# Keys spread by transfers, one bank of scores shared with POOL, and transposes moved in the queue

## The chip, the core and the metric

The kernel runs on one core of a Trainium2 chip. The metric is the device time of one execution in microseconds (us), lower is better. Three executions of the kernel before took 1627.0, 1628.25 and 1634.33 us, so the median is 1628.25 us. A fourth execution was profiled: it took 1626.31 us, of which 1624.5 us lie between its first and its last instruction (the span of the profile).

The five engines are named as the profile names them: PE (matrix products and transposes), DVE, ACT and POOL (elementwise work; POOL can't read the accumulators, DVE and ACT can), and SP, which here issues nearly all transfers. Each engine works through its own queue in order. All numbers are float32.

## The reference

Four layers follow each other on `x` of 128 batches by 64 tokens by 128 channels, with a second input of the same shape as context. The first three hold five attentions between them, all of the same form, with 16 heads of 8 channels (`HD`):

```python
def attend(q, k, v):                    # (batch, head, token, 8)
    a = softmax(einsum('bhnd,bhsd->bhns', q, k) * 8 ** -0.5, axis=-1)
    return einsum('bhns,bhsd->bhnd', a, v)
x = x + gate * (attend(q(xn), k(xn), v(xn)) @ proj + bias)   # "self", gated
x = x + attend(q(xn), k(c), v(c)) @ proj + bias              # "cross"
```

Layer 0 has a self attention (called L0s in the code), a cross attention (L0c) and an MLP; layer 1 is a cross attention with both sides modulated (L1c); layer 2 is self attention, cross attention (L2s, L2c) and MLP; layer 3 has attention with a single head and routed experts, and is not touched by the change.

## The kernel before

**Tiling.** The 8192 tokens are 16 groups of 512 (8 batches). `x` stays in SBUF (`xs`). Each attention runs over the 16 groups; L0s and L0c are one list of 32 groups, and L1c, L2s and L2c one list of 48, so that one attention runs into the next. A group is worked in two halves of four batches, `u = 0` and `u = 1`. Each half is one step of `attend` (line 571), so there are 160 halves.

**One half.** `scores` (468) makes the scores of 4 batches and 16 heads on PE: `sc`, 128 partitions by 2048, which fills four banks of PSUM. It has one buffer, so the next half's scores wait until this half's have been read. DVE takes the maximum over each row of 64 keys (`mx`, 485) and subtracts it (`e`, 487). `turned` (493) transposes half of `e` in 16 PE instructions into `pp`, two banks with one buffer, and ACT takes the exponential into `eT` (507). It is called twice in a half. `weighted` (509) multiplies by the values (`po`, 520), and ACT copies the product to `o` (528). A half passes through a pipeline: at each step the scores are of this half, the transposes of the last, the weighted sum of the one before.

**Preparation of a group** (`prepare`, 386) is a generator, cut into eight pieces by its `yield`s: load of context, statistics, normalization on POOL (372), transposes of the key input (`psT`, 342) with their evacuation by ACT (eight pieces of 128x64 where the layer modulates by batch, 359; otherwise one copy, 379), the same for the query input of a cross attention, keys, queries (`pq`, 449, to `qT`, 451), values (`pvv`, 459, to `vbd`, 464 and 465). The keys are `pk` (436), which ACT writes to `kT` (438); POOL then multiplies them by four masks (444) into `kbd`: of each block of 32 channels, that is 4 heads, `kbd[:, j]` holds the 8 channels of head `j` and zeros elsewhere. That lets one product per block of 32 rows give the scores of four heads.

**Finish of a group** (`finish`, 530) sends the denominators (which came out of `weighted` as additional columns of ones in `vbd`) through DRAM (`sums`, 538; `rc`, 542), moves the odd heads' rows of `o` beside the even ones by four transfers (545), takes reciprocals (547), sends them through DRAM (`recs`, 549) and back as one row per channel (`rb`, 554), multiplies on POOL (`oT`, 557), projects (`py`, 563) and adds to `x` (565, or 568 and 569 with a gate from the table `gt`, 278).

**What sets the order.** The order is written out by hand in `step` (588): after the first transposes and the weighted sum, an even step (`u = 0`) runs one piece of the finish of group i-2, of the preparation of i+4 and i+1 (keys), of the finish of i-3 (projection), then the second transposes, then a piece of the preparation of i+2 (`psT`) and i+3. On PE this gives for an even step: `sc`, `pp`, `po`, `pk`, `py`, `pp`, `psT`; for an odd one: `sc`, `pp`, `po`, `pq`, `pp`, `pvv`, and `psT` of the query input in a cross attention. Two PSUM buffers (pool `mm`, line 139) serve `po`, `pk`, `py`, `psT`, `pq` and `pvv` in turn. The first and last steps of a list are interleaved with the MLPs (`into_mlp`).

Of the kernel before, what the change touches and what calls it, by code (L numbers as in the profile page):

```python
# [15 lines left out]
P = 128  # L16
NST = 16
TT = 4
# [17 lines left out]
for _name, _n in _VECS:  # L36
# [13 lines left out]
    "L3_xcond_router_W": (3, 3), "L3_xcond_e_w1": (9, 256), "L3_xcond_e_w2": (6, 128),  # L50
    "L3_xcond_gate_w1": (3, 128), "L3_xcond_gate_w2": (1, 128), "L3_xcond_out_w": (1, 128),
}
_RAW = [
    "x", "cond_1024", "ctx_1024", *_WTS,
    "L0_xcond_ca_proj_b", "L1_xcond_bp", "L2_xcond_b_cproj", "L3_xcond_router_b", "L3_xcond_e_b2",
# [4 lines left out]
def tile_kernel(ctx: ExitStack, tc: tile.TileContext, a: dict, out: bass.AP):  # L60
# [15 lines left out]
    nc.sync.dma_start(cond, a["cond_1024"])  # L76
    vec_rows = const([_NVEC, P], "vec_rows")
    nc.scalar.dma_start(vec_rows, a["vecs"])
    mask = const([P, 4], "mask")
    nc.scalar.dma_start(mask, a["mask"])  # L80

    w = {}

    def load_weights(prefix, pool=cp):
        for name, (k, n) in _WTS.items():
            if name.startswith(prefix):
                t = pool.tile([P, k, n], F32, tag=name, name=name)
                src = a[name]
                if len(src.shape) == 3:
                    src = src.rearrange("e c n -> (e c) n")  # L90
                nc.sync.dma_start(t, src.rearrange("(k p) n -> p k n", p=P))
                w[name] = t

    xs = [const([P, TT, P], f"x{s}") for s in range(NST)]
# [23 lines left out]

    ident = const([P, P], "ident")
    make_identity(nc, ident)  # L120
    nhalf = const([P, TT], "nhalf")
    G.memset(nhalf, -0.5)

# [43 lines left out]
        Places.ak.tile([P, NB, 8, 32], F32, tag=f"vbd{i}", name=f"vbd{i}", bufs=1) for i in range(2)  # L167
    ]

    def clear(t):  # L170
        G.memset(t, 0.0)
        G.memset(t[0:L, :, :, 16:17], 1.0)
        G.memset(t[L:P, :, :, 17:18], 1.0)


# [2 lines left out]
    condT = const([P, P], "condT")  # L178
    scT = const([P, P], "scT")
    mods = {}  # L180

    def col(name, i=0):
        r = _ROW[name] + i
# [20 lines left out]

    def folded_column(wp, bp, bv, i):
        pb = mm("pb")
        T.matmul(pb[:, 0:1], w[wp][:, 0], col(bv, i), start=True, stop=True)
        t = const([P, 1], "pb_" + wp)
        V.tensor_add(t, pb[:, 0:1], col(bp))
        proj_bias[wp] = t  # L210
# [3 lines left out]
    def gate_table(wmod, wp, i=2, bias=None):  # L214

        table = dp.tile([P, 2, P], F32, tag="gate_" + wp, name="gate_" + wp)
        rows = const([P, 2, P], "gate_rows")
        gb = const([P, P], "gate_bias")
        V.tensor_scalar_mul(gb, mods[wmod][:, i, :], proj_bias[wp] if bias is None else bias)

        def second():
            pg = mm("pg")
            for q, src in enumerate((mods[wmod][:, i, :], gb)):
                T.transpose(pg[:, ts(q, P)], src, ident)
            V.tensor_copy(rows, pg[:, 0 : 2 * P].rearrange("p (i c) -> p i c", i=2))
            nc.sync.dma_start(table, rows)
            gates[wp] = table

        return second

    def folded_row(wp, bp, bv):
        bvs = const([P, P], "bvs")
        V.tensor_copy(bvs, col(bv, 1).broadcast_to([P, P]))

        def second():
            pb = mm("pb")
            T.matmul(pb[:, :P], bvs, w[wp][:, 0], start=True, stop=True)
            V.tensor_add(row_bias[bp], row_bias[bp], pb[:, :P])
            proj_bias[wp] = row_bias[bp]

        return second

    def condition():
        pc = mm("pc")
        T.transpose(pc[:, :P], cond, ident)
        V.tensor_copy(condT, pc[:, :P])
        S.activation(scT, pc[:, :P], AF.Silu)
        pv = mm("pv")
        T.transpose(pv[:, :_NVEC], vec_rows, ident[:_NVEC, :_NVEC])
        V.tensor_copy(vec, pv[:, :_NVEC])  # L250
        V.tensor_scalar_add(vec1, vec, 1.0)

    first_mods = modulations("L0_xcond_adaln_w", "L0_xcond_adaln_b", 6, (1, 4))
# [19 lines left out]
    def gate_tile(pool, s, wp):  # L273

        gt = pool.tile([P, TT, 2, P], F32, tag="gt", name="gt")
        for h in range(2):
            r = gates[wp].rearrange("(s t h) i c -> s h t (i c)", t=TT, h=2)[s, h]
            nc.sync.dma_start(
                gt[ts(h, L)].rearrange("p t i c -> p t (i c)"),
                r.unsqueeze(0).broadcast_to([L, TT, 2 * P]),  # L280
            )
        return gt

    later_tables = [
# [96 lines left out]

    turn = [0]

    ctxT = dp.tile([NST, P, NT], F32, tag="ctxT", name="ctxT")

    def prepare(pools, at):
# [16 lines left out]
        if cross:  # L403
            cn = c
            if layer != "L0c":
                cn = pool.tile([P, TT, P], F32, tag="cn", name="cn", bufs=1)
                for t in range(TT):
# [4 lines left out]
                    else:  # L412
                        S.activation(cn[:, t, :], c[:, t, :], AF.Identity, bias=nb, scale=rs)
        yield
        if layer == "L1c":
            kv_in = modulated_by_batch(pool, transposed(psum, cn), "L1_xcond_Wss_kv", 0, 1, s, "cm")
        elif cross:
            kv_in = copied(pool, transposed(psum, cn), "cm")
            if layer == "L0c":
                nc.sync.dma_start(ctxT[s], kv_in)  # L420
        else:
            q_in = kv_in = modulated_by_batch(
                pool, transposed(psum, xn), at["wmod"], 1, 0, s, by_dve=at.get("first", False)
            )
        yield
        if not cross:
# [12 lines left out]
        i = turn[0] % 2  # L439
        turn[0] += 1  # L440
        vbd = vbds[i]
        kbd = pool.tile([P, 4, NB, L], F32, tag="kbd", name="kbd")
        for j in range(4):
            (V if at.get("first") else G).tensor_scalar(  # L444
                kbd[:, j], by_batch(kT), mask[:, j : j + 1], 1.0, ALU.mult, ALU.mult
            )
        yield
        pq = psum.tile([P, 512], F32, tag="mm", name="pq")
        T.matmul(pq, at["wq"], q_in, start=True, stop=True)  # L449
# [11 lines left out]
                    start=True, stop=True,  # L461
                )
        pv4 = pvv.rearrange("p b (i d) -> p b i d", d=HD)
        S.copy(vbd[0:L, :, :, 0:HD], pv4[0:L])
        S.copy(vbd[L:P, :, :, HD : 2 * HD], pv4[L:P])
        at["vbd"] = vbd

    def scores(pools, at, u):
# [5 lines left out]
        for t2 in range(2):  # L474
# [9 lines left out]
        mx = pool.tile([P, 32], F32, tag="mx", name="mx")  # L484
        V.tensor_reduce(mx, sc.rearrange("p g (m k) -> p (g m) k", k=L), AX.X, ALU.max)  # L485
        e = pool.tile([P, 32, L], F32, tag="e", name="e")
        V.tensor_tensor(  # L487
            e, sc.rearrange("p g (m k) -> p (g m) k", k=L),
            mx.unsqueeze(2).broadcast_to([P, 32, L]), ALU.subtract,
        )  # L490
        return e

    def turned(pools, e, eT, gg):

# [35 lines left out]
    def finish(pools, at):  # L530
# [3 lines left out]
        cross = at["layer"][2] == "c"  # L534

        sums = dp.tile([16, NT], F32, tag="sums", name="sums", bufs=2)
        for j in range(2):
            nc.sync.dma_start(
                sums.rearrange("(g i j) t -> j g i t", i=2, j=2)[j], o[16 + j : P : 32, :, :]
            )  # L540
        rc = pool.tile([P, L], F32, tag="rc", name="rc")
        nc.sync.dma_start(rc, sums.rearrange("h (c t) -> (h c) t", t=L))

        for g in range(4):
            nc.sync.dma_start(o[32 * g + 16 : 32 * g + 32, 0, :], o[32 * g : 32 * g + 16, 1, :])
        yield
        V.reciprocal(rc, rc)
        recs = dp.tile([16, NT], F32, tag="recs", name="recs", bufs=2)
        nc.sync.dma_start(recs.rearrange("h (c t) -> (h c) t", t=L), rc)

        if not cross:
            gt = gate_tile(pool, s, at["wp"])
        rb = pool.tile([P, NT], F32, tag="rb", name="rb", bufs=1)
        nc.sync.dma_start(rb, recs.unsqueeze(1).broadcast_to([16, HD, NT]))
        yield
        oT = pool.tile([P, NT], F32, tag="oT", name="oT", bufs=1)
        G.tensor_tensor(oT, o[:, 0, :], rb, ALU.mult)  # L557
# [13 lines left out]
    def attend(pools, ats):  # L571
# [16 lines left out]
        def step(k, between=(), late=()):  # L588
            i, u = divmod(k, 2)
            now, last, past = (  # L590
                halves[k - d] if 0 <= k - d < 2 * n else None for d in range(3)
            )
            if now:
                now["e"] = scores(pools, now["at"], now["u"])
            for f in between:
                f()
            if last:
# [1 line left out]
                turned(pools, last["e"], last["eT"], 0)  # L599
            if past:  # L600
                weighted(pools, past["at"], past["u"], past["eT"])
            if u == 0:
                go(fin, i - 2)
                go(prep, i + 4)
                go(prep, i + 1)
                go(fin, i - 3)
            else:
                go(prep, i + 1)
            if last:
                turned(pools, last["e"], last["eT"], 1)  # L610
            if u == 0:
                go(prep, i + 2)
                go(prep, i + 3)
            else:
                go(prep, i + 1)
                go(prep, i + 2)
                for f in late:
                    f()
                go(fin, i - 1)
                go(fin, i - 2)  # L620
                go(prep, i + 4)
# [3 lines left out]
    def attention_of(s, layer):  # L625
        if layer[2] == "s":
            wmod, wqkv, bqkv, wp = {
                "L0s": ("L0_xcond_adaln_w", "L0_xcond_qkv_w", "L0_xcond_qkv_b", "L0_xcond_sa_proj_w"),
                "L2s": ("L2_xcond_W_mod", "L2_xcond_W_qkv", "L2_xcond_b_qkv", "L2_xcond_W_proj"),
            }[layer]  # L630
            m = w[wqkv][:, 0]
            return dict(
                s=s, layer=layer, wmod=wmod, wp=wp, wq=m[:, 0:P], bq=col(bqkv, 0),
                wk=m[:, P : 2 * P], bk=col(bqkv, 1), wv=m[:, 2 * P : 3 * P],
            )
        wq, bq, wkv, bkv, wp = {
            "L0c": (
# [8 lines left out]
        }[layer]  # L646
        m = w[wkv][:, 0]
        return dict(
            s=s, layer=layer, wp=wp, wq=w[wq][:, 0], bq=col(bq), wk=m[:, 0:P], bk=col(bkv, 0),
            wv=m[:, P : 2 * P],  # L650
        )

# [537 lines left out]
    def stages():  # L1190
# [41 lines left out]
        clear(vbds[0])  # L1232
        ahead_1(0, 1, 2, 3)
        condition()
        ahead_1(0, 0)
        first_mods[0]()
        ahead_1(0, 0, 1, 2, 0, 0, 1)
# [11 lines left out]
            f()  # L1249
        first_mods[2]()  # L1250
        n = last + 2 + len(heads_0)
        for f in steps_1[6:-n]:
            f()
        for s in range(2):
            heads_0[3 + s] = lambda s=s, f=heads_0[3 + s]: (f(), load_context(s))
        rest = into_mlp(steps_1, heads_0, turns_0)
# [68 lines left out]
```

## Time and profile before

| | before |
|---|---|
| profiled execution | 1626.31 us |
| its span, first to last instruction | 1624.5 us |
| median of three executions | 1628.25 us (1627.0 to 1634.33) |
| mean granted clock of PE | 0.997 |
| PE busy | 1573.8 us (97%) |
| DVE busy | 1240.4 us (76%) |
| POOL busy | 1072.5 us (66%) |
| ACT busy | 1035.5 us (64%) |
| transfers | 112.65 MB, 69 GB/s |

The attentions L0s and L0c stand between about 15 and 400 us, L1c, L2s and L2c between about 543 and 1120 us. The time from one even step's `sc` to the next (a pair of halves, that is, a group) is 11.92 us in L0s and L2s, 12.01 us in L0c, 12.25 us in L1c, and mostly 12.0 us in L2c, by the starts of `sc` in the timeline.

A row of the timeline gives the start in us, the duration in us, the engine, the line, the operation, the tiles written and read with their shapes, and how many instructions it merges; in brackets stands how long the engine was idle before it and what ended that. Busy time of PE is modelled for pipelined products, so it is read with the chain and the timeline, never alone.

### The profile page before, as it was taken

What the parts mean: (1) busy time and instruction counts of PE and PEld (TensorE: products, weight loads), DVE (VectorE), ACT (ScalarE), POOL (GpSimd) and SP (SyncE); (2) the same over time, 40 slices, a digit from 0 to 9 for tenths busy, and PEclk for the clock granted to TensorE, in tenths of its full rate; (3) what the DMA queues carried; (4) which work ended last, traced back from release to release, by engine and by line L of the source; (5) the groups of instructions that cost most, each with busy time, mean ns of one, the idle gap of its engine ahead of it and who ended that gap; (6) DMA issues with size and microseconds to landing.
All of it is one profiled execution on the core that took longest, in us unless ns stands there. A gap on an engine that the chain in (4) does not pass through costs nothing.

```text
span 1624.5 us, 64028 instructions
## 1 busy us (share of the span) xinstructions
PE 1573.8 (97%) x27842; PEld 1086.8 (67%) x27842; DVE 1240.4 (76%) x1566; ACT 1035.5 (64%) x1710; POOL 1072.5 (66%) x1786
## 2 busy tenths in 40 slices
PE   6999999998999899999999999998999999999998
PEld 4676777776544577776777777776777566666665
DVE  7898998898555688899899889896443566666666
ACT  5788777776433678878888888886334544444443
POOL 6687787766888789887787876775875333333322
PEclk9999999999999999999999999999999999999999
DMA  8334453332111022211334432222533111111100
GB/s 209 85 82 99 107 127 92 83 83 72 55 36 55 16 63 61 72 44 50 90 82 102 104 88 73 62 56 59 130 81 76 31 39 37 40 33 36 34 12 19
DMA packets 146775, 112.65 MB, mean 69 GB/s; under 512 B 36357, under 2 KB 125247, under 8 KB 146495
## 3 DMA queue, kind: packets, MB, share of 16 engines
q1 hardware_dynamic: 146288, 108.53, 26.1%
q8 instruction: 219, 3.59, 0.9%
q14 instruction: 61, 0.50, 0.1%
q10 hardware_dynamic: 207, 0.03, 0.0%
HBM read 83.99 MB, written 14.02 MB: 60 GB/s over the span
## 4 chain that ended last, share of the span: by engine, by line
PE 83%; DVE 12%; ACT 3%; issue 1%; DMA 0%; SPq 0%; DVEq 0%
PE sc L478 10%; PE pp L503 9%; PE po L520 7%; PE ph L693 7%; PE ph L1080 6%; PE ph L1081 6%; DVE e L487 6%; DVE mx L485 6%; PE po L1111 5%; PE psT L342 5%; PE pk L436 5%; PE py L563 4%; PE py L709 4%; PE py L699 3%; PE pvv L459 3%; PE pq L449 3%
## 5 line engine op out<-in xcount | busy, mean ns | idle before, releaser
L507 ACT ACTIVATE eT<-pp 128x1024 f32<-128x1024 f32 x320 | 329.7, 1030 | 160.8 <-PE pp L503 160.7
L485 DVE TENSOR_REDUCE mx<-sc 128x32 f32<-128x2048 f32 x160 | 366.6, 2291 | 83.6 <-PE sc L478 83.6
L487 DVE TENSOR_TENSOR e<-sc,mx 128x2048 f32<-128x2048 f32 x160 | 366.6, 2291 | 5.4
L503 PEld LDWEIGHTS pp<-ident,e 64*128 64x128 f32 x5120 | 183.9, 138 | 140.1 <-ACT eT L507 44.7
L503 PE MATMUL pp<-ident,e 64*128 64x64 f32 x5120 | 227.7, 229 | 7.2 <-DVE e L487 4.7
L444 POOL TENSOR_SCALAR kbd<-kT,mask 128x512 f32<-128x512 f32 x316 | 212.4, 690 | 31.3 <-ACT kT L438 28.3
L372 POOL TENSOR_SCALAR xn<-x,nmu,rs 128x128 f32<-128x128 f32 x508 | 223.6, 453 | 13.3
L557 POOL TENSOR_TENSOR oT<-o,rb 128x512 f32<-128x512 f32 x80 | 102.1, 1276 | 163.5 <-DMA rb<-recs 62.9
L478 PE MATMUL sc<-kbd,qT 32*64 32x256 f32 x5120 | 179.2, 387 | 16.6 <-DVE e L487 15.6
L694 ACT ACTIVATE h<-ph,vec 128x512 f32<-128x512 f32 x128 | 87.3, 687 | 149.9 <-PE ph L693 149.7
L520 PE MATMUL po<-eT,vbd 128*32 128x64 f32 x10240 | 178.1, 221 | 1.4 <-issue 1.3
L1087 ACT ACTIVATE h<-h 128x512 f32<-128x512 f32 x112 | 70.6, 630 | 149.8 <-DVE h L1083 130.9
L520 PEld LDWEIGHTS po<-eT,vbd 128*32 128x32 f32 x10240 | 151.3, 110 | 14.4 <-issue 2.0
L330 POOL TENSOR_TENSOR rs<-rs,nhalf 128x4 f32<-128x4 f32 x128 | 130.2, 1017 | 10.7
L478 PEld LDWEIGHTS sc<-kbd,qT 32*64 32x64 f32 x5120 | 97.7, 131 | 53.0 <-issue 19.6
L1083 DVE TENSOR_TENSOR h<-ph,ab 128x512 f32<-128x512 f32 x112 | 76.9, 687 | 62.6 <-PE ph L1081 62.5
L1116 DVE SCALAR_TENSOR_TENSOR acc<-po,pr,acc 128x128 f32<-128x128 f32 x192 | 67.2, 350 | 44.1 <-PE po L1111 39.6
L1080 PE MATMUL ph<-nx,w 128*128 128x512 f32 x192 | 100.7, 607 | 0.0
L528 ACT COPY o<-po 128x512 f32<-128x512 f32 x160 | 95.7, 598 | 5.1 <-PE po L520 2.0
L1081 PE MATMUL ph<-u,w_ev 128*128 128x512 f32 x192 | 98.9, 597 | 0.0
L1111 PEld LDWEIGHTS po<-w_2o,h 128*128 128x128 f32 x768 | 92.1, 192 | 8.7 <-issue 8.4
L1104 POOL TENSOR_SCALAR g<-g 128x512 f32<-128x512 f32 x16 | 9.9, 622 | 132.1 <-ACT g L1103 132.1
(259 smaller groups left out, 2868.5 us busy)
## 6 DMA issues: line engine op xcount, KB each, us to landing
rb<-recs SPq DMA_DIRECT2D x80, 256.0 KB
c<-in_ctx_dram SPq DMA_DIRECT2D x64, 256.0 KB
o<-o SPq DMA_DIRECT2D x320, 32.0 KB
gt<-gate_L_xcond_sa_proj_w SPq DMA_DIRECT2D x32, 256.0 KB
gt<-gate_L_xcond_W_proj SPq DMA_DIRECT2D x32, 256.0 KB
gt<-gate_L_xcond_W_mlp SPq DMA_DIRECT2D x32, 256.0 KB
x<-in_x_dram SPq DMA_DIRECT2D x16, 256.0 KB
ctxT<-cm SPq DMA_DIRECT2D x16, 256.0 KB
```

The source lines that it names most:

```text
L330: G.tensor_tensor(rs, rs, nhalf, ALU.pow)
L372: engine.tensor_scalar(xn[:, t, :], src[:, t, :], nmu[:, t : t + 1], rs[:, t : t + 1], ALU.add, ALU.mult)
L444: (V if at.get("first") else G).tensor_scalar(kbd[:, j], by_batch(kT), mask[:, j : j + 1], 1.0, ALU.mult, ALU.mult)
L478: T.matmul(sc[ts(h, L), g, ts(t2, 256)], qT[ts(g, 32), ts(b, L)], kbd[ts(g, 32), :, b, :], start=True, stop=True,)
L485: V.tensor_reduce(mx, sc.rearrange("p g (m k) -> p (g m) k", k=L), AX.X, ALU.max)
L487: V.tensor_tensor(e, sc.rearrange("p g (m k) -> p (g m) k", k=L), mx.unsqueeze(2).broadcast_to([P, 32, L]), ALU.subtract,)
L503: T.transpose(pp[:, h, ts(4 * g2 + 2 * i + t2, L)], e6[ts(h, L), 2 * gg + g2, t2, i], ident[ts(h, L), ts(h, L)],)
L507: S.activation(eT[:, gg], pp, AF.Exp, scale=HD ** -0.5)
L520: T.matmul(po[ts(g, 32), i, ts(2 * t2 + h, L)], at["vbd"][:, 4 * u + 2 * t2 + h, 2 * g + i, :], e7[:, g // 2, h, g % 2, i, t2, :], start=T ...
L1080: T.matmul(ps, wn, d["nx"], start=True, stop=False)
L1081: T.matmul(ps, we, d["u"], start=False, stop=True)
L1111: T.matmul(po[:, ex, :], d[q][:, ts(t, P)], k3["w_2o"][:, q, :], start=r == 0, stop=r == 1)
```

## The change

1. **Scores shared.** For every odd half, and for every half of L0c and L2c, DVE subtracts the maxima from three banks only (128x1536). A function `rest`, run after the weighted sum, has ACT copy the fourth bank from PSUM into `e`, and POOL subtract the maxima there in place.
2. **Keys spread by transfers.** POOL's four masked products are gone after the first two groups. The two `kbd` buffers are now fixed; the first two groups fill them with zeros and keys, and after that four transfers of 32 partitions by 2 KB, issued from SP as soon as `kT` is written, overwrite the rows that aren't zero. For this the heads of a block of 32 channels are interleaved (channel `g*32 + d*4 + j` for head `j`), so the columns of the query and key weights and their biases are reordered on the chip (`reorder`, by DVE for the first weights, by POOL for the others), and the values' columns and the projections' rows are interleaved by two.
3. **Fewer and other transfers in `finish`.** With that layout `o<-o` is one transfer instead of four, `sums<-o` one instead of two, `gt` one instead of two; `rb` is two instead of one.
4. **Order of an even step.** Keys (`prep, i + 1`) come first after the weighted sum. `finish` has one more `yield`, between the reciprocals and the loads of `gt` and `rb`, with the context's load of group i+4 between. The transposes `psT` of group i+2 go ahead of the second `pp`, and their evacuation stays behind it (a new `yield` under `in_two`).

The core of the diff:

```diff
+    kbds = [
+        Places.ak.tile([P, 4, NB, L], F32, tag=f"kbd{i}", name=f"kbd{i}", bufs=1) for i in range(2)
+    ]
...
+    def reorder(engine, name, n):
+        for i in range(n):
+            t = const([P, P], "gate_bias")
+            cols = w[name][:, 0, ts(i, P)]
+            engine.tensor_copy(t.rearrange("p (g d j) -> p g d j", d=HD, j=4), by_element(cols))
+            engine.tensor_copy(cols, t)
...
+    def spread(kbd, kT):
+        for j in range(4):
+            nc.sync.dma_start(kbd[j:P:4, j].rearrange("p b l -> p (b l)"), kT[j:P:4, :])
...
+        ps = transposed(psum, cn if cross else xn)
+        if at.get("in_two"):
+            at["open"] = True
+            yield
+            at["open"] = False
...
-        kbd = pool.tile([P, 4, NB, L], F32, tag="kbd", name="kbd")
-        for j in range(4):
-            (V if at.get("first") else G).tensor_scalar(
-                kbd[:, j], by_batch(kT), mask[:, j : j + 1], 1.0, ALU.mult, ALU.mult
-            )
+        kbd = kbds[i]
+        if turn[0] <= 2:
...
+        else:
+            spread(kbd, kT)
...
+        n = 24 if shared_with_pool(at, u) else 32
         V.tensor_tensor(
-            e, sc.rearrange("p g (m k) -> p (g m) k", k=L),
-            mx.unsqueeze(2).broadcast_to([P, 32, L]), ALU.subtract,
+            e[:, 0:n], sc[:, 0 : n // 8].rearrange("p g (m k) -> p (g m) k", k=L),
+            mx[:, 0:n].unsqueeze(2).broadcast_to([P, n, L]), ALU.subtract,
         )
-        return e
+
+        def rest():
+            if n < 32:
+                S.copy(e[:, n:32], sc[:, 3].rearrange("p (m k) -> p m k", k=L))
+                G.tensor_tensor(
+                    e[:, n:32], e[:, n:32],
+                    mx[:, n:32].unsqueeze(2).broadcast_to([P, 32 - n, L]), ALU.subtract,
+                )
+
+        return e, rest
+
+    def shared_with_pool(at, u):
+        return u == 1 or at["layer"] in ("L0c", "L2c")
...
-        for g in range(4):
-            nc.sync.dma_start(o[32 * g + 16 : 32 * g + 32, 0, :], o[32 * g : 32 * g + 16, 1, :])
+        nc.sync.dma_start(o[1:P:2, 0, :], o[0:P:2, 1, :])
...
+            if rest:
+                rest()
             if u == 0:
+                go(prep, i + 1)
                 go(fin, i - 2)
                 go(prep, i + 4)
-                go(prep, i + 1)
+                go(fin, i - 2)
                 go(fin, i - 3)
+                if i + 2 < n:
+                    ats[i + 2]["in_two"] = True
+                go(prep, i + 2)
             else:
                 go(prep, i + 1)
             if last:
                 turned(pools, last["e"], last["eT"], 1)
             if u == 0:
-                go(prep, i + 2)
+                if i + 2 < n and ats[i + 2].get("open"):
+                    go(prep, i + 2)
                 go(prep, i + 3)
...
+        reorder(V, "L0_xcond_qkv_w", 2)
         ahead_1(0, 0)
```

## The prediction

> **What bounds the kernel now.** I read first the chain of work that ended last, then the costliest groups, then the timeline of one pair of halves in each attention.
>
> ```profile
> PE 83%; DVE 12%; ACT 3%; issue 1%; DMA 0%; SPq 0%; DVEq 0%
> ```
>
> PE carries the chain; DVE has 12%, about 195 us, and the chain in order of time puts these into odd halves of the self attentions. So POOL's time is off the path, and DVE's counts only where a half waits for `e`.
>
> ```profile
> L485 DVE TENSOR_REDUCE mx<-sc 128x32 f32<-128x2048 f32 x160 | 366.6, 2291 | 83.6 <-PE sc L478 83.6
> L487 DVE TENSOR_TENSOR e<-sc,mx 128x2048 f32<-128x2048 f32 x160 | 366.6, 2291 | 5.4
> L444 POOL TENSOR_SCALAR kbd<-kT,mask 128x512 f32<-128x512 f32 x316 | 212.4, 690 | 31.3 <-ACT kT L438 28.3
> L557 POOL TENSOR_TENSOR oT<-o,rb 128x512 f32<-128x512 f32 x80 | 102.1, 1276 | 163.5 <-DMA rb<-recs 62.9
> L528 ACT COPY o<-po 128x512 f32<-128x512 f32 x160 | 95.7, 598 | 5.1 <-PE po L520 2.0
> ```
>
> These give the prices: 2.29 us for a subtraction of 2048 columns, 0.60 for an ACT copy of a bank, 1.28 for a POOL operation of that shape. Now the timeline of one pair in L0s, cut to the instructions that pace it:
>
> ```profile
> 161.29 1.12 PE L478 MATMUL sc<-kbd,qT 32*64 32x256 f32 x32 [0.17 <-DVE e L487]
> ...
> 165.98 0.71 PE L503 MATMUL pp<-ident,e 64*128 64x64 f32 x16
> ...
> 166.62 0.66 PE L342 MATMUL psT<-ident,xn 128*128 128x128 f32 x4
> 166.74 1.02 ACT L507 ACTIVATE eT<-pp 128x1024 f32<-128x1024 f32 x1 [0.87 <-PE pp L503]
> ...
> 167.66 2.47 ACT L359 ACTIVATE xm<-psT,mod_L_xcond_adaln_w 128x64 f32<-128x64 f32 x8
> ...
> 170.18 1.12 PE L449 MATMUL pq<-xm,L_xcond_qkv_w 128*128 128x512 f32 x2 [0.17 <-ACT xm L359]
> 170.76 2.29 DVE L487 TENSOR_TENSOR e<-sc,mx 128x2048 f32<-128x2048 f32 x1
> 171.34 0.76 ACT L451 ACTIVATE qT<-pq,vec 128x512 f32<-128x512 f32 x1
> ...
> 173.20 1.12 PE L478 MATMUL sc<-kbd,qT 32*64 32x256 f32 x32 [0.17 <-DVE e L487]
> ```
>
> The pair takes 11.91 us. Two chains end nearly together: DVE's `e` (170.76 + 2.29 = 173.05), and `pp`, `eT`, `xm` on ACT, `pq`, which waits for `xm` because it takes the PSUM buffer of `psT`; behind it `pp` and `pvv` would end near 173.0. In L0c:
>
> ```profile
> 245.32 1.12 PE L478 MATMUL sc<-kbd,qT 32*64 32x256 f32 x32
> ...
> 248.87 2.29 DVE L487 TENSOR_TENSOR e<-sc,mx 128x2048 f32<-128x2048 f32 x1
> ...
> 250.65 0.66 PE L342 MATMUL psT<-ident,c 128*128 128x128 f32 x4
> ...
> 251.54 0.63 DVE L565 TENSOR_TENSOR x<-x,py 128x512 f32<-128x512 f32 x1
> ...
> 256.74 0.66 PE L342 MATMUL psT<-ident,xn 128*128 128x128 f32 x4
> ```
>
> Here the chain is PE alone, 12.01 us a pair: no relief of DVE can help.
>
> **The change, part by part.** Times are from the start of the even half's `sc`.
>
> *What DVE saves.* A subtraction of 1536 columns costs 2.29 x 3/4 = 1.72 us (between 1.5 and 1.9), so 0.57 less. By itself it lets the odd half of a self attention end by 0.2 us sooner, when the other chain comes in: at most 30 pairs x 0.2 = 6 us. In L0c, L2c and L1c it is worth nothing.
>
> *What the ACT copy costs.* 112 copies of 0.60 us would fit ACT's 64%. But the built program has the copy wait for DVE's subtraction of the same half, which is the first to write the tile `e`. And ACT works in order: behind the copy stand `kT` (even half) or `qT` (odd half). In an odd half starting at S, the maximum starts at S+1.22 and the subtraction at S+3.55 (rows above), ends at S+5.27; the copy runs to S+5.9, `qT` (starts 0.5 after a queued copy, lasts 0.69 to 0.76) to S+6.5. The next `sc` reads `qT`, and in a cross attention `psT` must first take `pq`'s buffer, which `qT` frees, and lasts 0.58. So an odd half is at least 6.55 us in a self attention (now 5.99) and 7.13 in a cross one (now 6.09 in L0c, 6.33 in L1c).
>
> *The moved transposes.* Ahead of the second `pp` they push it back 0.59 us, the step from `psT` to `sc`; nothing on PE waits there before (in L0s `pp` starts 165.98, right behind `py`). `eT`, `xm` and `pq` come 0.59 later. In L0s that alone would make the pair 11.69 + 0.59 = 12.3, in L1c 12.25 + 0.59 = 12.85; there the copy's chain is longer, and covers it. In L0c and L2c it costs more. `psT` stands right behind `py` and, by the built program, takes `py`'s PSUM buffer, so it waits for DVE's `x<-x,py`. DVE works it off behind `e` and the reciprocal: before, it ended at 251.54 + 0.63 - 245.32 = 6.85, less 0.57 is 6.28. PE is ready for `psT` at 4.69. Behind it stand `psT` 0.59 and `pp` 0.64, so the odd `sc` starts at 6.33 + 1.23 = 7.56 instead of 5.92. The odd half then takes its 7.13. A pair is 14.7 us against 12.0: **+2.7**.
>
> A rule of the Trainium skill bears on the copy: PSUM — Partial Sum Buffer, Terms, says that no two engines may access one PSUM bank at once, reads included. By it alone the copy could start when the maximum has been read, before the subtraction ends; only the transposes' cost would then be left. No run here shows that start, and I go by the program's wait.
>
> *Keys by transfers.* POOL loses 4 x 0.69 us and gains 1.28 a shared half; it had slack, so 0. The trace doesn't show these transfers. Issue: `o<-o`, the nearest row, takes 0.51 to 1.82 us, median 0.59, so four take 2.0 to 7, 2.4 likely. Landing: from `sums` issued to `rc` issued is 2.1 us, from `rb` issued to `oT` 3.4 to 6.3. `kT` ends at 4.6 (6.5 in L0c), so keys lie ready at 9 to 13; `sc` needs them at 12.5 (14.7). I take 2.1, hence 0, with 0 to 1 us a pair as bounds. What is queued behind on SP: the four hold back `recs`, `c`, `gt` and `rb`. `recs` goes from 6.3 to 7.1 in self attentions (9.0 in L0c), and `rb` is 0.55 longer. `oT` before ended 0.4 to 1.4 us ahead of `py` in L0s and 1.2 to 3 in L0c; the longer pair gives back 0.6 and 2.7. So it lies near zero: 0 to 0.5 us a pair, I take 0. The single `o<-o` frees about 1.8 us of SP ahead of the keys, where SP had time. The moved context load is in front of `rb`, but its 0.6 us run while `rb` waits for `recs` to land.
>
> *Start.* DVE reorders the first weights ahead of the first statistics. These weights are issued at 2.19; the weights issued at 1.64 let PE start at 5.80, so 6.35; four copies of 0.29 (the `condT` row's shape) bring the statistics from 4.69 to 7.5. All up to the first `sc` at 15.7 hangs on it: **+2.9** (0.4, if only the small copies count, to 3.5). POOL's reorders, 16 x 0.45, lie in the time of masks that it no longer does.
>
> **Sum.** The pairs next to a change of layer prepare the other kind of group, and the last two of L0c and L2c overlap the MLP.
> - L0s: 13 x 0.6 + 2 x 1.1 = 10
> - L0c: 14 x 2.7 + 2 x 1.4 = 40.6
> - L1c: 14 x 0.83 + 2 x 0.6 = 12.8 (5.92 + 7.13 = 13.05 against 12.25 gives about 0.8)
> - L2s: as L0s, 14 pairs, 10.6
> - L2c: as L0c, 40.6; ACT's `cn`, 1.65, ends before the copy's chain does
> - Start: 2.9
>
> 117.5 us on the profiled 1626.31 is 1743.8. The runs' median is 1.9 above the profiled execution; I forecast **1745**.
>
> **Rivals.**
> *The copy isn't held* (it can leave early enough that `qT` isn't late): the odd halves keep only the transposes' cost. Self 28 x 0.37 (12.29 against 11.92), L1c 14 x 0.59, L0c and L2c 30 x 1.7, start 2.9: 10 + 8 + 51 + 3 = 72, so **1698**. For it speaks that ACT is 64% busy; against it the program's wait and ACT's order.
> *Transfers late:* `rb` lands at its slow end, `py` waits in each pair and every engine behind it: 0.5 us more on 80 pairs, 40 us, **1785**. For it: `oT` already waits 62.9 us for `rb` in total, and `py` 13.9 behind `oT`.
> *Faster:* PE's own work sets the pair everywhere, 11.41 us in self attentions, 12.0 in cross ones. It decides if, in odd halves, `qT` leaves ACT before PE has done `pvv`, and if `psT` finds its buffer free at 4.69. Then 30 x 0.5 + 16 x 0.25 - 3 = 16 us are won: **1610**. Against it: both waits stand in the program, and ACT's `xm` would have to come earlier, not later.
> *It does nothing:* the DVE time is won where PE is the bound, and both waits are covered; gain and start cancel: **1625**.
>
> **How the numbers follow.** Forecast 0.74, copy not held 0.12, transfers late 0.09, faster 0.03, nothing 0.02. The forecast's own spread is about 25 us to each side (0.25 us in the 2.7, on 30 pairs, and the bounds of the transfers and the start). The range, 1695 to 1787, takes in most of the two neighbours too, and leaves out about 0.15. With 0.5%, about 8 us, as what a measurement of this kernel can tell from no change: faster 0.03, same 0.02, slower 0.95.
>
> **What would show it.** In the profile after: subtractions of 1.72 us; PE idle ahead of `psT` in L0c and L2c for about 1.6 us, ended by DVE's `x<-x,py`; PE idle ahead of the query's `psT` or of `sc`, ended by ACT's `qT`; ACT idle ahead of the copy, ended by DVE's `e`; halves of 7.6 and 7.1 us in L0c and L2c; pairs of 12.5 in self attentions and 13.1 in L1c; DVE's share of the chain above 20%. Pairs of 12.0 in L0c would refute the wait for `x<-x,py`; an odd half of 6.1 with the copy's end long before `qT` would refute the copy's chain; `sc` waiting for transfers, or `py` for `oT`, would put the loss on SP.

## The result, and the profile after

The changed kernel takes 2009.02 us (median of four, 2007.67 to 2011.83) against 1628.39 us before: a ratio of 1.2331 (95% interval 1.2298 to 1.2364), 381 us more. The forecast was 1745 us (1695 to 1787). The direction was right; the size was not. The profiled execution has a span of 2006.4 us, and PE's mean granted clock fell from 0.997 to 0.935. Times below are medians, or the one execution there was; of x5_gt_four (below), one of two executions had a lower granted clock than the other (1938.55 us at 0.841, against 0.973) and is left out.

The chain of work that ended last, on the page of the changed kernel:

```profile
PE 41%; DMA 26%; DVE 16%; POOL 6%; ACT 5%; issue 4%; SPq 2%; ACTq 0%; DVEq 0%; POOLq 0%
DMA rb<-recs 16%; DVE mx L554 7%; DVE e L557 5%; PE sc L547 5%; PE ph L1169 5%; PE ph L1170 5%; DMA gt<-gate_L_xcond_W_mlp 5%; PE po L1200 4%; PE psT L397 3%; PE py L644 3%; DMA sums<-o 3%; PE ph L782 3%; PE pp L585 3%; PE py L788 3%; PE po L602 2%
```

Transfers, which carried nothing before, now carry 26% of the chain, some 520 us: `rb`, the gate table of the last MLP, and `sums`. DVE rose to 16%, not to the "above 20%" of the prediction, because the chain moved to the queue (without the slow transfer, in x1_gt_two below, it is 24%). The groups that answer to those shown of before:

```profile
L554 DVE TENSOR_REDUCE mx<-sc 128x32 f32<-128x2048 f32 x160 | 366.6, 2291 | 311.0 <-PE sc L547 307.6
L557 DVE TENSOR_TENSOR e<-sc,mx 128x1536 f32<-128x1536 f32 (+1 forms) x160 | 306.8, 1917 | 5.4
L564 ACT COPY e<-sc 128x512 f32<-128x512 f32 x112 | 65.5, 585 | 156.1 <-DVE e L557 156.1
L638 POOL TENSOR_TENSOR oT<-o,rb 128x512 f32<-128x512 f32 x80 | 101.6, 1271 | 238.7 <-DMA rb<-recs 228.2
```

DVE's subtractions are 60 us shorter in sum (306.8 against 366.6), and none of it is seen in the time. ACT's copy waits 156 us for them: 1.4 us ahead of each. POOL's `oT` waits 228 us for `rb` (62.9 before). The waits of SP's queue, and of DVE, say the same of two other transfers (columns: us in total, times, longest us):

```profile
SPq L621 <- DMA sums<-o: 387.1, 80, 11.2
```

```profile
DVE y L808 <- DMA gt<-gate_L_xcond_W_mlp: 95.2, 13, 13.3
```

Before, the wait for `sums` was 131.2 us. By stages, from the first `sc` of one to the first of the next (the stretches after L0c and L2c include what follows them):

| stretch | before | predicted | measured | of it with two gate transfers (x1_gt_two) |
|---|---|---|---|---|
| up to the first `sc` | 15.7 | +2.9 | +2.5 | +2.7 |
| L0s | 193.5 | +10 | +93.8 | +16.4 |
| L0c and the MLP behind it | 333.5 | +40.6 | +62.0 | +46.1 |
| L1c | 195.1 | +12.8 | +15.7 | +15.7 |
| L2s | 192.2 | +10.6 | +95.9 | +13.2 |
| L2c, MLP, layer 3 | 694.5 | +40.6 | +112.0 | +46.9 |

L1c has no gate and came out near what was worked out. What is missing lies where a gate tile is loaded: in L0s, in L2s, in the first pairs behind each, and in the MLP of L2. In the timeline of a pair in L2s of the changed kernel:

```profile
1003.05 0.58 SPq L333 DMA_DIRECT2D gt<-gate_L_xcond_W_proj  x1
1004.17 1.26 SPq L635 DMA_DIRECT2D rb<-recs  x2
1009.03 0.59 SPq L619 DMA_DIRECT2D sums<-o  x1
1017.23 1.26 POOL L638 TENSOR_TENSOR oT<-o,rb 128x512 f32<-128x512 f32 x1 [5.92 <-DMA rb<-recs]
1017.29 0.32 SPq L621 DMA_DIRECT2D rc<-sums  x1
1018.28 2.45 SPq L443 DMA_DIRECT2D kbd<-kT  x4
1018.55 2.08 PE L644 MATMUL py<-L_xcond_W_proj,oT 128*128 128x128 f32 x8 [3.87 <-POOL oT L638]
1021.52 0.59 SPq L333 DMA_DIRECT2D gt<-gate_L_xcond_W_proj  x1
```

`rb` is issued at 1004.17 and `oT` can start at 1017.23, 13 us later (5.0 before); `rc`, which waits for `sums` of 1009.03, is issued in the same moment. Two transfers with nothing in common arrive together: both stood behind a third, `gt`, issued at 1003.05.

SP's queue and its transfers alone give the pair its length. From the issue of `gt` to that of `rc` there are 14.4 us (median in L2s). From there SP issues `rc`, `o`, the four key transfers and `recs` almost without a pause, and after 4.2 us (median) comes the next `gt`. From one `gt` to the next it is 19.0 us in the median, and as long takes a pair from the fifth on.

### The profile page after: what moved, and what is told of

It reads as the page before. It is cut to its first block, busy times and chain, and to the rows that moved or that the text cites. A ratio compares the mean times of both kernels' runs of the same rounds, so it can differ in the third digit from the quotient of the medians.

```text
span 2006.4 us, 64051 instructions
## 1 busy us (share of the span) xinstructions
PE 1675.1 (83%) x27844; PEld 1146.1 (57%) x27844; DVE 1188.6 (59%) x1575; ACT 1083.8 (54%) x1822; POOL 985.4 (49%) x1602
## 4 chain that ended last, share of the span: by engine, by line
PE 41%; DMA 26%; DVE 16%; POOL 6%; ACT 5%; issue 4%; SPq 2%; ACTq 0%; DVEq 0%; POOLq 0%
DMA rb<-recs 16%; DVE mx L554 7%; DVE e L557 5%; PE sc L547 5%; PE ph L1169 5%; PE ph L1170 5%; DMA gt<-gate_L_xcond_W_mlp 5%; PE po L1200 4%; PE psT L397 3%; PE py L644 3%; DMA sums<-o 3%; PE ph L782 3%; PE pp L585 3%; PE py L788 3%; PE po L602 2%
## 5 line engine op out<-in xcount | busy, mean ns | idle before, releaser
L554 DVE TENSOR_REDUCE mx<-sc 128x32 f32<-128x2048 f32 x160 | 366.6, 2291 | 311.0 <-PE sc L547 307.6
L557 DVE TENSOR_TENSOR e<-sc,mx 128x1536 f32<-128x1536 f32 (+1 forms) x160 | 306.8, 1917 | 5.4
L565 POOL TENSOR_TENSOR e<-e,mx 128x512 f32<-128x512 f32 x112 | 116.8, 1043 | 368.3 <-ACT e L564 368.3
L585 PEld LDWEIGHTS pp<-ident,e 64*128 64x128 f32 x5120 | 197.6, 148 | 163.1 <-ACT eT L589 99.0
L585 PE MATMUL pp<-ident,e 64*128 64x64 f32 x5120 | 243.0, 239 | 12.8 <-ACT eT L589 8.8
L427 POOL TENSOR_SCALAR xn<-x,nmu,rs 128x128 f32<-128x128 f32 x508 | 223.7, 453 | 13.2
L547 PE MATMUL sc<-kbd,qT 32*64 32x256 f32 x5120 | 199.8, 424 | 30.2 <-ACT qT L520 20.6
L602 PEld LDWEIGHTS po<-eT,vbd 128*32 128x32 f32 x10240 | 154.6, 112 | 12.6 <-DVE mv L368 1.5
L564 ACT COPY e<-sc 128x512 f32<-128x512 f32 x112 | 65.5, 585 | 156.1 <-DVE e L557 156.1
L547 PEld LDWEIGHTS sc<-kbd,qT 32*64 32x64 f32 x5120 | 102.3, 143 | 69.1 <-ACT qT L520 27.0
L397 PE MATMUL psT<-ident,xn 128*128 128x128 f32 x512 | 90.0, 304 | 35.6 <-ACT qT L520 29.6
L625 DVE RECIPROCAL rc<-rc 128x64 f32<-128x64 f32 x80 | 43.8, 547 | 99.3 <-DMA rc<-sums 99.3
L397 PEld LDWEIGHTS psT<-ident,xn 128*128 128x128 f32 x512 | 66.4, 155 | 61.4 <-ACT qT L520 35.7
```

Source lines behind the costliest of these rows:

```text
L397: T.transpose(ps[:, ts(t, P)], src[:, t, :], ident)
L427: engine.tensor_scalar(xn[:, t, :], src[:, t, :], nmu[:, t : t + 1], rs[:, t : t + 1], ALU.add, ALU.mult)
L547: T.matmul(sc[ts(h, L), g, ts(t2, 256)], qT[ts(g, 32), ts(b, L)], kbd[ts(g, 32), :, b, :], start=True, stop=True,)
L557: V.tensor_tensor(e[:, 0:n], sc[:, 0 : n // 8].rearrange("p g (m k) -> p (g m) k", k=L), mx[:, 0:n].unsqueeze(2).broadcast_to([P, n, L]), ...
L565: G.tensor_tensor(e[:, n:32], e[:, n:32], mx[:, n:32].unsqueeze(2).broadcast_to([P, 32 - n, L]), ALU.subtract,)
L585: T.transpose(pp[:, h, ts(4 * g2 + 2 * i + t2, L)], e6[ts(h, L), 2 * gg + g2, t2, i], ident[ts(h, L), ts(h, L)],)
```

## The experiments

### Which transfer is late

Theory G: the gate tile. The change loads it by one transfer of 128 partitions whose source is two rows, each read 64 times; before it was two transfers of 64 partitions. Rival K: the key transfers, or the two strided `rb`. **x1_gt_two** changes the gate alone:

```diff
-        nc.sync.dma_start(
-            gt.rearrange("p t i c -> p (t i c)"),
-            r.unsqueeze(1).broadcast_to([2, L, TT * 2 * P]),
-        )
+        for h in range(2):
+            nc.sync.dma_start(
+                gt[ts(h, L)].rearrange("p t i c -> p (t i c)"),
+                r[h].unsqueeze(0).broadcast_to([L, TT * 2 * P]),
+            )
```

> The changed kernel with one edit: the gate tile is loaded by two transfers of 64 partitions each, as before the change, in place of one of 128 partitions whose source is two rows, each read 64 times. The layout of the gate table in memory stays as the change made it. Theory G (the single gate transfer is slow, and everything behind it on the queue comes late): the self attentions' pairs go from 17.5 to 22 us to the 12.5 of the changed kernel's first three L2s pairs, which come before any gate is in the queue; L0c stays at 14.9, L1c at 13.1; about 80 us less in L0s, 85 in L2s, 30 in the first pairs of L0c and L2c, 55 in the MLP of L2: 1755 us (1740 to 1775). Rival K (the spread keys, or the reciprocals' two transfers, are what comes late): nothing changes, 1960 to 2015 us.

Measured: 1767.1 us, ratio 1.0852 (1.0834 to 1.087), 242 us less. Self pairs 12.6, L0c 14.88, L1c 13.11; the MLP of L2 as before. G holds, and the same two rows are still read 64 times each, so it is not the repeated reading that is slow. **x2_gt_copies** keeps one transfer of 512 KB, and has it read 16 rows eight times each:

```diff
-            r.unsqueeze(1).broadcast_to([2, L, TT * 2 * P]),
+            r.unsqueeze(1).broadcast_to([16, L // 8, TT * 2 * P]),
```

> The changed kernel with the gate tile still loaded by one transfer of 128 partitions and 512 KB, but its source holds 16 rows, each read 8 times, in place of 2 rows, each read 64 times: every row of the gate table lies eight times in memory, written at the start by 48 transfers in place of 6. Theory G1 (the transfer is slow because its source's outermost loop counts 2, so that only two DMA engines work at it): as with two transfers, 1760 us (1740 to 1790, some microseconds of it for the more writes at the start). G2 (one transfer of 512 KB is slow by its size, or by being one): 1950 to 2020 us. K: 1960 to 2020 us.

Measured: 1773.94 us, one execution. A single transfer of 512 KB is as fast as two; what matters is the count of the source's outermost loop (G1). **x5_gt_four** takes four rows:

> The changed kernel, the gate tile still loaded by one transfer of 128 partitions and 512 KB, its source four rows, each read 32 times (every row lies twice in memory). In the MLP of L2 of the changed kernel, with two source rows, gates landed 10.0 us apart when nothing else was waited for. Theory G1 (as many DMA engines work as the outermost loop of the source counts): 5 us a transfer in place of 10, less than a pair or a sequence of the MLP takes, so nearly all the loss is gone: 1780 us (1760 to 1830). Rival G2 (a shared source row is slow to read however many engines there are): 1950 to 2015.

Measured: 1834.88 us in one execution, 5 us above the range of G1 and over 100 below that of G2. G1 expected nearly all of the loss to go, and it did not: a transfer of half the time still stands ahead of `rb` and `sums` in each pair. From `rb`'s issue to `oT` (median, L2s from the fifth pair on) there are 13.2 us with two rows, 8.2 with four, 5.1 with sixteen, 4.7 with two transfers; some pairs of x5_gt_four take 12.6 us and some 16.5.

**x4_before_gt_one** puts the single gate transfer (with the table's layout) into the kernel before, and **x3_masks** gives the changed kernel POOL's masks back (this is the edit of x3_masks):

```diff
-        if turn[0] <= 2:
-            for j in range(4):
-                ... (masks)
-        else:
-            spread(kbd, kT)
+        for j in range(4):
+            ... (masks)
```

> The kernel before with one edit of the change alone: the gate table laid out so that both tokens' halves are contiguous, and the gate tile loaded by one transfer with two source rows. Theory G: the stalls of the changed kernel appear in L0s, L2s and the MLP of L2, with the clock falling too: 1840 us (1780 to 1900). K: 1620 to 1640 us.

Measured: 1889.28 us, one execution. The gate transfer alone costs the kernel before 262 us.

> The changed kernel with the keys' block form made by POOL's four multiplications by a mask again, and no transfers of keys; all else of the change stays. Theory G: the gate transfer is unchanged, so the time stays within 30 us of 2009. Rival K (four transfers of keys for each pair are what comes late, or hold the queue): 1730 to 1800 us.

Measured: 1956.89 us, one execution. Not the bulk, so K falls, but 52 us where theory G allowed 30. With the queue the bound, each issue less counts: in L2s `rc` still goes 14.4 us behind `gt`, but the next `gt` follows after 2.9 us in place of 4.2.

The speed can be read in the MLP of L2 of the changed kernel, where `y` waits for nothing but gates:

```profile
1525.93 0.69 DVE L808 TENSOR_TENSOR y<-py,gt 128x512 f32<-128x512 f32 x1 [13.32 <-DMA gt<-gate_L_xcond_W_mlp]
1535.91 0.69 DVE L808 TENSOR_TENSOR y<-py,gt 128x512 f32<-128x512 f32 x1 [4.79 <-DMA gt<-gate_L_xcond_W_mlp]
1545.89 0.69 DVE L808 TENSOR_TENSOR y<-py,gt 128x512 f32<-128x512 f32 x1 [4.07 <-DMA gt<-gate_L_xcond_W_mlp]
```

They land 9.98 us apart: 524,288 bytes in 9.98 us is 53 GB/s, 26 GB/s for each of two engines. That they are two can be read where SP issues nothing else (columns: window, its length, busy us and instructions of PE, PEld, DVE, ACT, POOL, then granted clock, mean DMA share of 16 engines, GB/s):

```profile
1526.00:1546.00 20.00, 15.43 (x73) 11.35 (x74) 8.71 (x22) 4.01 (x6) 11.48 (x19) 0.83 0.13 54
```

0.13 of 16 engines is 2.1. The Trainium skill, DMA: Bandwidth & Descriptors, "Why a DMA increments its semaphore by 16 and not by 1", has this rule: a transfer gets the largest number up to 16 that divides the slowest loops of both its sides, so two here. The page's Specifications give about 27 GiB/s an engine; an estimate from that is 9.0 us, where 9.98 was measured.

### What the other edits cost

The next four start from x1_gt_two. **y1_no_share** has DVE subtract all four banks; **y2_back** puts the transposes back behind the second `pp`; **y3_neither** does both.

```diff
 y1_no_share
-        return u == 1 or at["layer"] in ("L0c", "L2c")
+        return False
 y2_back
-                if i + 2 < n:
-                    ats[i + 2]["in_two"] = True
-                go(prep, i + 2)
...
-                if i + 2 < n and ats[i + 2].get("open"):
-                    go(prep, i + 2)
+                go(prep, i + 2)
```

> The kernel with two gate transfers (x1_gt_two), and DVE subtracts all four banks again in every half: no copy by ACT, no subtraction by POOL. The transposes stay ahead of the second pp. Theory B (both edits cost, as the prediction has them: the copy holds qT and kT back on ACT, the transposes wait for DVE's x<-x,py in L0c and L2c): self pairs 12.3, L1c 12.85; in L0c and L2c x<-x,py ends 0.57 later, so the even half is 8.2, the odd one 6.1, a pair 14.3 in place of 14.88; 1740 us (1725 to 1750). Rival T (the transposes alone cost, the copy is free): 1757 to 1770. Rival C (the copy alone costs): 1630 to 1650.

Measured: 1668.99 us (1.025, 1.0219 to 1.0282), near none of the theories. Self pairs 12.2 and L1c 12.78 are as expected; but L0c is 12.09, not 14.3. What B had wrong stands in the timelines. First the changed kernel in L0c, then y1_no_share, in the even half:

```profile
402.99 0.58 ACT L564 COPY e<-sc 128x512 f32<-128x512 f32 x1 [1.98 <-DVE e L557]
403.28 0.63 DVE L646 TENSOR_TENSOR x<-x,py 128x512 f32<-128x512 f32 x1
403.47 0.69 ACT L504 ACTIVATE kT<-pk,vecp 128x512 f32<-128x512 f32 x1
403.96 0.66 PE L397 MATMUL psT<-ident,c 128*128 128x128 f32 x4 [1.68 <-DVE x L646]
```

```profile
327.68 0.69 ACT L505 ACTIVATE kT<-pk,vecp 128x512 f32<-128x512 f32 x1 [0.40 <-PE pk L503]
328.42 0.66 PE L398 MATMUL psT<-ident,c 128*128 128x128 f32 x4
```

With the copy, `kT` is late, and the program gives `psT` the buffer of `py`: it starts when `x<-x,py` ends (403.91). Without the copy `psT` gets the buffer of `pk`, which `kT` has read by 328.37, and waits for nothing. The semaphores agree: in eleven L0c pairs of each trace, this `psT` waits for DVE in the changed kernel and in y2_back, and for ACT in y1_no_share, y3_neither and y4_back_copy_late. So the wait for `x<-x,py` belongs to a copy ahead of `kT`, not to the place of the transposes.

> The kernel with two gate transfers, bank sharing kept as the change has it, and the transposes put back behind the second pp. Theory B: the self pairs stay at 12.5 and L1c near 13.05, since the copy's chain sets them; in L0c and L2c the even half no longer waits for x<-x,py, but kT stands behind the copy, and the transposes behind kT, so both halves are 7.1, a pair 14.2: 1745 us (1735 to 1760). T: 1630 to 1650. C: 1757 to 1770.

Measured: 1745.76 us (1.0723, 1.0693 to 1.0754), pairs 12.69, 13.13 and 14.24: the numbers are theory B's. Its way is not, in the even half of L0c: `psT`, now behind the second `pp`, still waits for `x<-x,py`, and starts before `kT` ends (336.33).

```profile
335.64 0.69 ACT L505 ACTIVATE kT<-pk,vecp 128x512 f32<-128x512 f32 x1
336.13 0.66 PE L398 MATMUL psT<-ident,c 128*128 128x128 f32 x4 [0.65 <-DVE x L647]
```

> Two gate transfers, no sharing, transposes behind the second pp: what is left of the change are the key transfers, the interleaved channels, the fewer transfers at a group's end and the reorders at the start. Theory B: pairs as before the change (11.9, 12.0, 12.25), the start 2.9 longer: 1631 us (1626 to 1645). Rival L (the key transfers hold the queue so that the reciprocals land late, 0.5 us a pair): 1660 to 1675.

Measured: 1653.5 us (1.0159, 1.012 to 1.0197): neither, but nearer to L. About half of the pairs are as before, most of the others 0.1 to 1.8 us longer.

**y4_back_copy_late** is y2_back with `rest()` moved behind `go(prep, i + 1)` in both kinds of half:

> As y2_back, sharing kept, but ACT's copy is issued behind kT (even halves) and qT (odd ones) in place of ahead of them: the same instructions, another order on ACT alone. Theory B (what costs is what stands behind the waiting copy): self pairs 12.0, L0c and L2c 12.0 to 12.3, L1c 12.3: 1640 us (1628 to 1660). Rival W (the copy costs by itself, since the scores' PSUM tile is free only when it has ended, or since POOL's part comes late): within 15 us of y2_back, 1730 to 1760.

Measured: 1670.08 us (1.0262, 1.0228 to 1.0296), 76 us less than y2_back by the order on ACT alone, 10 us above B's range and far from W's. Self pairs 12.12, L1c 12.37; L0c is 12.52, 0.2 above what B allowed. An odd half of L0c, in y2_back and then in y4_back_copy_late:

```profile
342.12 0.58 ACT L565 COPY e<-sc 128x512 f32<-128x512 f32 x1 [1.96 <-DVE e L558]
342.60 0.69 ACT L521 ACTIVATE qT<-pq,vecp 128x512 f32<-128x512 f32 x1
343.35 0.66 PE L398 MATMUL psT<-ident,xn 128*128 128x128 f32 x4 [1.06 <-ACT qT L521]
```

```profile
323.97 0.69 ACT L521 ACTIVATE qT<-pq,vecp 128x512 f32<-128x512 f32 x1 [0.44 <-PE pq L519]
325.48 0.58 ACT L565 COPY e<-sc 128x512 f32<-128x512 f32 x1 [0.82 <-DVE e L558]
325.59 0.66 PE L398 MATMUL psT<-ident,xn 128*128 128x128 f32 x4
```

Behind the copy, `qT` is late and `psT` waits for it; ahead of the copy it is early. What stays is of W's kind: `eT` and `vbd` now stand behind the copy on ACT, and in L0c `po` waits 0.28 us for `vbd`; in other places, mostly self attentions, the next `sc` waits for the copy (9.8 us of PE's idle time in all).

### Keys by transfers, and the sharing alone

**y5_neither_masks** is y3_neither with POOL's masks. **y8_recs_first** is y3_neither with the finish of i-2 (`recs`) ahead of the keys of i+1, and so `recs` ahead of the key transfers on SP:

```diff
-                go(prep, i + 1)
                 go(fin, i - 2)
                 go(prep, i + 4)
+                go(prep, i + 1)
```

> As y3_neither (two gate transfers, no sharing, transposes behind the second pp), with the keys' block form made by POOL's masks again, so that no keys go through the queue. y3_neither's 25 us over the kernel before are the start and late reciprocals in single pairs. Theory Q (four key transfers stand on SP's queue ahead of recs, which goes at 7.1 to 7.6 us of a pair in place of 6.3, so that rb lands late): 1633 us (1628 to 1640), what is left being the start. Rival F (the two strided transfers of rb, of 64 rows each with 8 source rows, are what lands late): 1645 to 1658.

Measured: 1630.99 us (1.0018, 1.0006 to 1.003), as theory Q has it: the key transfers cost 22.5 us.

> As y3_neither, keys by transfers, but the group's reciprocals are sent (recs) ahead of the next group's key transfers in SP's order, as they stood before the change. Theory Q: most of the loss returns, 1638 us (1630 to 1646). Rival F, or a Q2 in which the key transfers cost by their traffic and not by their place: 1647 to 1660.

Measured: 1691.26 us (1.0385, 1.0348 to 1.0423), 38 us worse instead of 15 better. `recs` did go early; but `rb` did not. SP's queue in y3_neither, with the pair's `sc` at 828.86, and in y8_recs_first, with it at 835.13:

```profile
833.46 2.91 SPq L444 DMA_DIRECT2D kbd<-kT  x4
836.48 0.52 SPq L628 DMA_DIRECT2D recs<-rc  x1
837.05 1.14 SPq L334 DMA_DIRECT2D gt<-gate_L_xcond_W_proj  x2
838.29 1.26 SPq L636 DMA_DIRECT2D rb<-recs  x2
```

```profile
841.44 0.33 SPq L628 DMA_DIRECT2D recs<-rc  x1
841.88 3.32 SPq L444 DMA_DIRECT2D kbd<-kT  x4
845.25 1.23 SPq L334 DMA_DIRECT2D gt<-gate_L_xcond_W_proj  x2
846.59 0.62 SPq L636 DMA_DIRECT2D rb<-recs  x1
```

The four key transfers hold SP for 2.9 and 3.3 us here (medians in L2s 2.4 and 2.9). Ahead of `recs` they lie partly in the wait for DVE's reciprocal; behind it they push back `rb`. `rb`'s issue stands at 8.5 us of an L2s pair in y5_neither_masks, 10.2 in y3_neither and 11.4 in y8_recs_first (medians); PE idles 1.4, 11.5 and 32.3 us ahead of `py` for `oT`, and the times are 1631, 1653.5 and 1691. So it is `rb`'s place that the time follows, and Q named the wrong instruction. Why the issues run longer in y8_recs_first stays open.

**y9_share_no_queue** is y4_back_copy_late with the masks, the sharing alone:

> As y4_back_copy_late (bank sharing kept, ACT's copy behind kT and qT, transposes behind the second pp, two gate transfers), with the keys by POOL's masks, so that no keys go through the queue: the sharing alone, in its best order. Theory S (the copy follows DVE's subtraction, so 1.76 + 0.59 is no shorter than 2.29, and the next sc waits for the copy): y5_neither_masks plus the 16.6 us by which y4_back_copy_late exceeds y3_neither, 1648 us (1640 to 1656); self pairs 12.1, L0c 12.5. Rival P (the sharing pays where DVE is in the way, once the queue no longer is): 1615 to 1627, self pairs 11.4 to 11.8.

Measured: 1657.53 us (1.018, 1.0157 to 1.0204), self pairs 12.12, L0c 12.52. The size is 1.5 us above S's range, the mechanism is S's: ahead of `sc` PE idles 14.1 us for the copy, where without sharing it idled 13.9 for DVE's subtraction. Another 9.9 us ahead of `po`, for `vbd`, are new. So the sharing costs 26.5 us over y5_neither_masks in the best order tried, and gains nothing anywhere. No version was found that beats the kernel before.

Undoing the edits one by one gives the whole difference:

| edit undone | from | to | us |
|---|---|---|---|
| single gate transfer | 2009.0 (after) | 1767.1 (x1_gt_two) | 241.9 |
| a bank shared | 1767.1 | 1669.0 (y1_no_share) | 98.1 |
| transposes ahead of the second `pp` | 1669.0 | 1653.5 (y3_neither) | 15.5 |
| keys by transfers | 1653.5 | 1631.0 (y5_neither_masks) | 22.5 |
| what is left (reorders, layout, fewer transfers, order of keys and context) | 1631.0 | 1627.6 (before, x1's runs) | 3.4 |

In the other order the sharing is 92.3 (y2_back to y3_neither) and the transposes 21.3 (x1_gt_two to y2_back).

## Why the prediction was wrong

**The step that failed** is the account of SP's queue: "the four hold back `recs`, `c`, `gt` and `rb`", with "0 to 0.5 us a pair, I take 0". It counted `gt` as something that waits, at its issue time. The sum has no term for its rewritten load, which was put at nothing without a reason. The runs show 242 of the 381 us there: two engines carry it, and `rb` and `sums` land behind it. The prediction's own sign for a loss on SP, `py` waiting for `oT`, is in the timeline (3.87 us). The rival *transfers late* had the right victim (`rb` lands late, `py` waits, every engine behind it) but not the cause, and a price of 0.5 us a pair; measured in L2s were 5 to 8 us (pairs of 17.7 to 20.6 against 12.6). The page of before allowed an estimate: 108.53 MB in 26.1% of 16 engines' 1624.5 us is 16 GB/s an engine, so the two engines would need up to 16 us for 512 KB, more than a pair.

**What DVE saves, in cross attentions nothing:** right, and in self attentions it was nothing too.

**The ACT copy:** right in mechanism, and in the length of the halves. The copy starts when DVE's subtraction ends (402.99), `kT` and `qT` come behind it, the odd half of L0c is 7.2 us (7.13 worked out), self pairs are 12.5 to 12.6 (12.5), L1c 13.1 (13.05). y4_back_copy_late shows that it is ACT's order.

**The moved transposes:** the time was right (even half 7.67 against 7.56, pair 14.88 against 14.7, wait 1.68 against 1.6), the blame was not. y1_no_share and y4_back_copy_late show that the wait for `x<-x,py` is there only with the copy ahead of `kT`; moving the transposes costs 15 to 21 us in all.

**Keys by transfers:** taken at 0; 22.5 us measured, 0.28 us a pair, inside the bounds of 0 to 0.5. They delay `rb`, as the bound said, and no wait of `sc` for them is among those of y3_neither's profile.

**Start:** 2.9 worked out, 2.5 measured.

**The clock** had no term. In the changed kernel PE is busy 1675.1 us, 1602.5 in x1_gt_two with as many products, so the lower clock makes PE's work 73 us longer. That is no share of the 242 us beside the waiting: in L2s SP's queue and its transfers give the pair its length, and PE has no part in that loop. For the MLP this was not worked out.

With the gate's load as before, the change takes 1767 us, inside the forecast's range. The split behind that number is partly luck. Copy and transposes together cost 113.6 us, and the forecast's sum gives them 114.6; but the prediction put most of the 2.7 us of L0c and L2c on the transposes, and the runs put 98 of the 113.6 on the sharing. The 22.5 us of the keys come on top.

## What to carry to other kernels

Of a rewritten transfer, compare the loop counts of both its sides with the old ones, not the bytes or the number of issues: here a tidier single transfer, its source's outermost loop counting 2 in place of 64, took 10 us and made whatever was issued behind it late, though nothing waited for the tile itself in the attentions. When two unrelated transfers land at the same moment, look for the one issued ahead of both. Work taken off DVE was worth nothing here: what replaced it stood in ACT's queue ahead of what the next half reads, and with that order mended `sc` waited for the copy in place of the subtraction.

## What the runs showed of the hardware

PE's granted clock by stretches, in the changed kernel: L2s before the first gate is loaded, then the rest of L2s; below, a stretch of the same L2s pairs in x1_gt_two (columns as in the line of 1526.00 above):

```profile
911.00:950.00 39.00, 35.37 (x933) 25.48 (x928) 31.13 (x25) 31.05 (x59) 20.12 (x31) 1.00 0.22 69
950.00:1193.00 243.00, 170.84 (x3816) 124.07 (x3820) 132.42 (x100) 127.49 (x234) 102.28 (x142) 0.85 0.21 73
```

```profile
857.00:1017.00 160.00, 146.22 (x3794) 105.00 (x3786) 128.53 (x99) 126.72 (x233) 100.94 (x141) 1.00 0.36 107
```

About as many products take 170.8 us in place of 146.2. After the idle time of 3.87 us in the timeline above, `py` takes 2.08 us (1.08 in L0c), and the products are back at their usual times at 1025.1, 6.6 us later; the waits of 1.68 us in L0c leave `psT` at 0.66. The Trainium skill, TensorE: Matmul & The Clock Gate, "What's actually happening", puts the gate at an idle window of about 3.4 us and half the clock behind it; these rows agree. A row of x3_masks does not quite: there `py` takes as long behind an idle time of only 2.74 us, so by this row less than the page's window was enough.

```profile
989.33 2.08 PE L641 MATMUL py<-L_xcond_W_proj,oT 128*128 128x128 f32 x8 [2.74 <-POOL oT L635]
```

From the changed kernel's `py` to the next `pp` (1024.39) four groups of products take 5.84 us; their usual times (1.08, 0.66, 0.71, 1.12) sum to 3.57, so at the slower clock PE needs at least 2.3 us more here.

The profile's mean DMA share hides this kind of bound: it reads 0.21 in the stretch that waits for transfers, and 0.36 in the one without these waits. Only where the slow transfer is alone can the two engines be read from it (0.13 above).
